# A shared expert with its weights held in the array and 512 tokens moving, and softmax sums collected in 128 columns

## The chip, the cores and the metric

The kernel runs on one core of one Trainium2 chip. The metric is the device time of one execution in microseconds (us), of which the median of several runs is given. All data are float32.

## What is computed

A transformer block for 2048 tokens of width 512. Its output is the input plus two branches, both of which read the layer-normalised input `xn`:

```
x  = query                                    # 2048 x 512
xn = layernorm(x)
# attention: 16 heads, two score matrices of depth 16 each, causal
a1, a2 = softmax(mask(q1 k1^T / 4)) v, softmax(mask(q2 k2^T / 4)) v      # v is 32 wide
f  = lowpass over tokens (a1 - lambda a2)     # filter in the frequency domain
attn = (rmsnorm per head(f) * const) @ Wout
# mixture of experts: 8 routed experts of width 352, the best 2 per token, and a shared one of width 704
routed = sum over the 2 chosen e:  w_e * ((silu(xn w1_e) * (xn w3_e)) @ w2_e)
shared = (silu(xn sw1) * (xn sw3)) @ sw2
out = x + attn + routed + shared
```

## The kernel before

Tokens lie in 16 tiles of 128. `xnT` holds the normalised input transposed (width on the partitions, in four chunks of 128, tokens along the free axis), `vd` the values. The work stands in three stages.

**First stage** (to about 259 us in the profile). Layer norm, transposes and the values; gating (which scatters a list `who` with 32 indirect DMAs, L400); the projections of queries and keys, which are written to memory as `parts_q` and `parts_k`; and last the shared expert for the first four token tiles (`EARLY = 4`), whose results go to memory as `ysh` (L199) on POOL's queue.

**Middle** (`middle`, 259 to 1313 us). Attention in 32 turns: 8 groups of two heads times 4 chunks of 512 queries. A turn is a list of units; a unit is one block of 128 keys for one head: two score matmuls (`ps_s`, L689), an exp on ACT over 128x1024 (`pt`, L702), and for both heads together four value matmuls into 32 columns each (`ps_o`, L733) and additions on DVE that collect the exps (`sum`, L743). When a turn has ended, `sums` adds `sum` over its partitions with matmuls against ones (`ps_sum`, L753), DVE copies the result (`s_sb`), and one step later `finish` transposes outputs and sums (`ps_ot`, `ps_st`, four transposes each) and DVE divides. Keys and queries come back from memory as `kS` (L597) and `qS` (L609) on SP's queue: four `kS` and eight `qS` transfers are needed for the first unit pair of the first turn.

Between the units, the generator `experts()` puts expert work into PE's queue: first the shared expert for token tiles 4 to 14, then 36 blocks of the routed experts. Each `yield` gives its cost by hand, and the loop takes as many steps as keep `worked / work_all` level with the share of attention units done. In this stage the order of PE, POOL and SP is the order in which the program is written; DVE and ACT are ordered by a scheduler.

**Ending** (1313 to 1432 us). The filter as matmuls on folded values (`ps_z`), the shared expert for the last token tile (`kept`), rms norm on DVE, the output projection (`po`), and sums of all parts by accumulating DMAs on POOL's queue.

**The shared expert before** is treated as two halves of width 352, each like a routed expert. For one token tile and one half, `up_first` does 4 matmuls (the tile's 128x128 chunks of `xnT` are the weights in the array, 352 columns of sw1 move; `xh`), a tanh on ACT and a DVE step that make silu; `up_third` does 4 more matmuls for sw3 (`xg`) and a product on DVE. The hidden values then lie with tokens on the partitions, so `turned_back` transposes them (three transposes, `ps_u`, L180, and two DVE copies, `uT`) before `down` multiplies with sw2 (`xy`, L190, 3 matmuls of 512 columns for each half). One float32 matmul is two PE instructions.

**Branches.** A branch on a flag `more` (L1140), whose body does up to three more routed blocks, stands in the text between the first stage and the middle; the scheduler places it into the streams. On the path where its body is not run, each engine only raises its counters by what the body would have raised. A second branch (L1157, `calm`) chooses between two forms of the middle; this input takes the first.

Matmul results go to `PSUM` banks of a pool `fps` with three buffers in the middle, which expert work, `ps_sum`, `ps_ot` and `ps_st` share in turn.

Of the kernel before, what the change touches and what calls it, by code (L numbers as in the profile page):

```python
# [8 lines left out]
F32 = mybir.dt.float32  # L9
# [10 lines left out]
P = 128  # L20
# [13 lines left out]
NF = len(FCH)  # L34
TOP = 2
# [24 lines left out]
def block_kernel(  # L60
# [41 lines left out]
    nc.vector.memset(ones, 1.0)  # L102
    calm = cpool.tile([1, 1], I32, name="calm")
# [34 lines left out]
    def expert(mp, fps, stores=2):  # L138


# [55 lines left out]
        def stored(y, dst, scale, eng=nc.sync):  # L196
            y_sb = mp.tile([P, E], F32, tag="y_sb", name="y_sb", bufs=stores)
            nc.vector.tensor_scalar(y_sb, y, scale, None, ALU.mult)  # L198
            eng.dma_start(dst, y_sb)  # L199
# [4 lines left out]
        return up_first, up_third, up, turned_back, (down, down_products, stored), transposed  # L204


    with ExitStack() as pools:
# [213 lines left out]
        _, _, up, turned_back, (down, _, _), _ = expert(ep, eps, EARLY)  # L421
# [49 lines left out]
        early = None  # L471
        for t in range(EARLY):
            xT = xnT[:, :, t * P : (t + 1) * P]
            u0 = up(w_sb[0][0], xT)
            if t == 0:
                pm = lps.tile([P, 2, P], F32, tag="x", name="ps_most")
                for i in range(2):
                    nc.tensor.transpose(pm[:1, i, :], most[:, i : i + 1], ident)
                line = l1.tile([1, 2], F32, name="line")
                nc.vector.tensor_reduce(line, pm[:1], AX.X, ALU.max)  # L480
                prod = l1.tile([1, 1], F32, name="prod")
                nc.vector.tensor_mul(prod, line[:, 0:1], line[:, 1:2])
                nc.vector.tensor_scalar(calm, prod, BOUND / (D * SCALE), None, ALU.is_le)
            else:
                early.append(turned_back(u1))
            u1 = up(w_sb[1][0], xT)
            if t > 0:
                down([(w[1], uT) for w, uT in zip(w_sb, early)], ysh[t - 1], 0.5, nc.gpsimd)
            early = [turned_back(u0)]
        early.append(turned_back(u1))  # L490
        down([(w[1], uT) for w, uT in zip(w_sb, early)], ysh[EARLY - 1], 0.5, nc.gpsimd)

    def middle(general):


        with ExitStack() as pools:
# [23 lines left out]
            up_first, up_third, _, turned_back, (down, _, _), transposed = expert(mp, fps)  # L520

            def experts():


                late = None
                for t in range(EARLY, NT - 1):
                    last = t == NT - 2
                    xT = xnT[:, :, t * P : (t + 1) * P]
                    half = up_first(w_sb[0][0], xT)
                    if t == NT - 3:  # L530
                        who_sb = mp.tile([NR, P, 2], F32, tag="who", name="who_sb", bufs=1)
                        nc.sync.dma_start(who_sb, who[: NR * P, :].rearrange("(n p) o -> n p o", p=P))
                    yield 2.4
                    u = up_third(w_sb[0][0], xT, half)
                    if last:


                        xr = [rows_of(0), rows_of(1)]
                        es = [routed(0)]
                        fetch_up(es[0], 0, nc.sync)  # L540
                    yield 2.4
                    uTs = [turned_back(u)]
                    half = up_first(w_sb[1][0], xT)
                    yield 2.9
                    u = up_third(w_sb[1][0], xT, half)
                    if last:
                        es.append(routed(1))
                        fetch_up(es[1], 1, nc.sync)
                    yield 2.4
                    if late is not None:  # L550
                        down(*late)
                    uTs.append(turned_back(u))
                    late = [(w[1], uT) for w, uT in zip(w_sb, uTs)], ysh[t], 0.5
                    if t == NT - 3:
                        ps = bank([P, 2, NR], "ps_w")
                        for i in range(2):
                            nc.tensor.transpose(ps[:, i, :], who_sb[:, :, i], ident[:NR, :NR])
                        nc.vector.tensor_copy(tok, ps[:, 0, :])
                        nc.vector.tensor_copy(wcol, ps[:, 1, :])
                    if last:  # L560
                        xT = transposed(xr.pop(0))
                    yield 5.7 if t > EARLY else 0.5
                for j in range(NR):
# [9 lines left out]
                    down(*late)  # L573
                    if j == 0:
                        fetch_down(es[0], 0, nc.sync)
                    fetch_down(es[j + 1], (j + 1) % 2, nc.sync)
# [82 lines left out]
            class Chunk:  # L659
# [88 lines left out]
                def sums(self):  # L748
                    ps = bank([P, QC], "ps_sum")
                    for h in range(2):  # L750
                        for s in range(2):
                            r = 64 * h + 32 * s
                            nc.tensor.matmul(  # L753
                                ps[r : r + 32, :], ones[:, :32], self.sum[h][:, s, :], start=True, stop=True,
                                skip_group_check=True,
                            )
                    self.s_sb = ap.tile([P, QC], F32, tag="s_sb", name="s_sb", bufs=1)
                    nc.vector.tensor_copy(self.s_sb, ps)

                def finish(self):  # L760
                    po = bank([P, TQ, 4, 32], "ps_ot")
                    psum = bank([P, TQ, 4, 32], "ps_st")
# [3 lines left out]
                    for i in range(TQ):  # L766
                        c = slice(i * P, (i + 1) * P)
                        nc.tensor.transpose(psum[:, i].rearrange("p a d -> p (a d)"), self.s_sb[:, c], ident)
                    r = ap.tile([P, TQ, 2, 2], F32, tag="rcp", name="rcp")
                    nc.vector.reciprocal(r.rearrange("p t h s -> p t (h s)"), psum[:, :, :, 0])  # L770
# [74 lines left out]
            work_all = (NT - 1 - EARLY) * 15.8 + NR * 8.5 - 7.0  # L845
# [78 lines left out]
    def ending():  # L924
# [3 lines left out]
        with tc.tile_pool(name="tail1", bufs=1) as t1, tc.tile_pool(name="tail", bufs=2) as tp, tc.tile_pool(  # L928
# [7 lines left out]
            up_first, up_third, _, turned_back, (_, down_products, stored), _ = expert(tp, fps)  # L936
# [67 lines left out]
            u = up_third(w_sb[0][0], kept, up_first(w_sb[0][0], kept))  # L1004
# [9 lines left out]
            uTs = [turned_back(u)]  # L1014
# [92 lines left out]
            half = up_first(w_sb[1][0], kept)  # L1107
# [3 lines left out]
            u = up_third(w_sb[1][0], kept, half)  # L1111
            pairs.append(prepared(1))
            uTs.append(turned_back(u))
            pairs[0].means()
            y = down_products([(w[1], uT) for w, uT in zip(w_sb, uTs)])
# [90 lines left out]
def _experts(w1, w3, w2, sw1, sw3, sw2):  # L1206
# [4 lines left out]
    halves = [slice(i * FI, (i + 1) * FI) for i in range(2)]  # L1211
    w1 = [*w1, *(sw1[:, h] for h in halves)]
    w3 = [*w3, *(sw3[:, h] for h in halves)]
    w2 = [*w2, *(sw2[h] for h in halves)]
    a = np.zeros((NX + 2, P, WCOL), np.float32)
    for e in range(NX + 2):
        up = a[e, :, : NE * 2 * FI].reshape(P, NE, 2, FI)
        for i, w in enumerate((w1[e], w3[e])):
            up[:, :, i] = w.reshape(NE, P, FI).transpose(1, 0, 2)
        for ic, (i0, m) in enumerate(FCH):  # L1220
            o = NE * 2 * FI + ic * E
            a[e, :m, o : o + E] = w2[e][i0 : i0 + m]
    return a
# [34 lines left out]
```

## Time and profile before

| | us |
|---|---|
| median of 3 runs (lowest to highest) | 1432.54 (1431.59 to 1432.81) |
| the profiled execution | 1433.46 |
| its span, from first to last instruction | 1431.7 |

| engine | busy us | share of the span |
|---|---|---|
| PE (matmul) | 1359.2 | 95% |
| DVE | 1073.6 | 75% |
| ACT | 660.7 | 46% |
| POOL | 568.7 | 40% |

The profile is of one execution. A group of instructions is given as line, engine, operation and tiles (output<-inputs), its shape and its count; a count of PE is of instructions, twice the matmuls for float32. "Idle before" is the time its engine waited, with what ended the wait. PEld is the loading of weights into the array, which overlaps matmuls; SPq and POOLq are the queues that issue DMAs.

### The profile page before, as it was taken

How to read it: one execution, taken by the hardware profiler on the slowest of the kernel's cores; microseconds unless marked ns; L12 is line 12 of the kernel's file. 1: busy time of each engine (PE TensorE's matmuls, PEld its weight loads, DVE VectorE, ACT ScalarE, POOL GpSimd, SP SyncE). 2: the span in 40 equal slices, each digit the busy share in tenths (PEclk: the TensorE clock that was granted, in tenths of full speed). 3: DMA queues.
4: the chain of work that ended last, by engine and by line, in shares of the span. 5: the costliest groups of instructions: out<-in, count | busy, mean ns of one | idle time of the engine just before them, and what ended most of it. 6: DMA issues, size and time to landing. Idle time of an engine off the chain costs nothing.

```text
span 1431.7 us, 19747 instructions
## 1 busy us (share of the span) xinstructions
PE 1359.2 (95%) x6968; PEld 637.4 (45%) x6968; DVE 1073.6 (75%) x1489; ACT 660.7 (46%) x780; POOL 568.7 (40%) x668
## 2 busy tenths in 40 slices
PE   7999999899999999999999999999989999999998
PEld 3444455344444443444444444444434444444443
DVE  7058872577777777777787889788879878887785
ACT  2211110455545545555565565556646546552221
POOL 0002222011301131136964754556548536623773
PEclk9999999999999999999999999999999999999999
DMA  9306661210101110236566656465566564546996
GB/s 378 145 15 206 185 197 33 74 56 33 61 28 37 38 62 14 60 126 177 181 190 180 218 179 185 143 208 180 157 177 198 185 179 157 174 153 234 194 223 147
DMA packets 74636, 206.51 MB, mean 144 GB/s; under 512 B 12012, under 2 KB 12176, under 8 KB 69152
## 3 DMA queue, kind: packets, MB, share of 16 engines
q1 hardware_dynamic: 61840, 177.62, 38.4%
q0 software_dynamic: 11168, 23.17, 8.0%
q10 hardware_dynamic: 1520, 4.36, 0.9%
q8 instruction: 58, 0.95, 0.3%
q14 instruction: 50, 0.41, 0.1%
HBM read 161.26 MB, written 43.85 MB: 143 GB/s over the span
## 4 chain that ended last, share of the span: by engine, by line
PE 58%; DVE 10%; POOL 5%; issue 5%; ACT 4%; DMA 3%; SPq 0%; ACTq 0%; DVEq 0%; POOLq 0%
PE ps_o L733 14%; PE ps_s L689 10%; PE xh L156 9%; PE xg L156 9%; PE xy L190 8%; DVE sum L743 4%; ACT pt L702 3%; PE ps_sum L753 2%; POOL pt L707 2%; DMA wd<-in_wex_dram 1%; PE po L1095 1%; DMA wu<-in_wex_dram 1%; PE ps_u L180 1%; DVE y_sb L198 1%; PE ps_ot L765 1%
## 5 line engine op out<-in xcount | busy, mean ns | idle before, releaser
L743 DVE TENSOR_TENSOR sum<-sum,pt 128x1024 f32<-128x1024 f32 (+3 forms) x576 | 627.4, 1123 | 111.9 <-ACT pt L702 61.7
L702 ACT ACTIVATE pt<-ps_s 128x1024 f32<-128x1024 f32 x544 | 533.6, 1026 | 256.8 <-PE ps_s L689 217.4
L707 POOL TENSOR_SCALAR_AFFINE_SELECT pt<-pt 128x256 f32<-128x256 f32 x256 | 160.3, 649 | 366.6 <-ACT pt L702 365.5
L733 PE MATMUL ps_o<-pt,vd 128*32 128x512 f32 (+3 forms) x2560 | 271.6, 542 | 1.9 <-POOL pt L707 1.9
L689 PE MATMUL ps_s<-qS,kS 64*128 64x512 f32 (+3 forms) x1280 | 214.5, 416 | 18.8 <-ACT pt L702 18.8
L190 PE MATMUL xy<-wd,uT 128*128 128x512 f32 (+1 forms) x408 | 186.8, 599 | 1.9 <-DMA wd<-in_wex_dram 1.5
L689 PEld LDWEIGHTS ps_s<-qS,kS 64*128 64x128 f32 x1280 | 100.3, 186 | 196.2 <-ACT pt L702 94.3
L733 PEld LDWEIGHTS ps_o<-pt,vd 128*32 128x32 f32 x2560 | 67.6, 110 | 133.8 <-issue 118.7
L782 POOL TENSOR_TENSOR vd<-o_n 128x128 f32<-128x128 f32 x62 | 34.9, 583 | 205.0 <-DVE o_n L773 144.7
L400 POOL DMA_INDIRECT who<-pairs,slot x32 | 36.2, 1132 | 196.5 <-DVE pairs L397 106.5
L190 PEld LDWEIGHTS xy<-wd,uT 128*128 128x128 f32 (+1 forms) x408 | 74.6, 190 | 86.5 <-issue 74.7
L446 PE MATMUL ps_x<-xnT,wqk_sb 128*128 128x512 f32 x256 | 110.5, 593 | 0.0
L163 ACT ACTIVATE xtanh<-xh 128x352 f32<-128x352 f32 x68 | 31.6, 464 | 146.1 <-PE xh L156 134.3
L156 PE MATMUL xh<-wu,xT 128*128 128x352 f32 x288 | 93.6, 468 | 1.3 <-DMA wu<-in_wex_dram 0.7
L156 PE MATMUL xg<-wu,xT 128*128 128x352 f32 x288 | 93.4, 467 | 0.0
L156 PE MATMUL xg<-wu,xnT 128*128 128x352 f32 x240 | 77.3, 464 | 0.8 <-DVE xtanh L164 0.6
L156 PE MATMUL xh<-wu,xnT 128*128 128x352 f32 x240 | 77.0, 464 | 1.0 <-DVE rcp L770 1.0
L149 ACT COPY xT<-ps_x 128x512 f32<-128x512 f32 x36 | 21.1, 586 | 118.6 <-PE ps_x L147 118.6
L446 PEld LDWEIGHTS ps_x<-xnT,wqk_sb 128*128 128x128 f32 x256 | 48.4, 190 | 60.6 <-issue 60.6
L156 PEld LDWEIGHTS xg<-wu,xT 128*128 128x128 f32 x288 | 52.7, 190 | 35.8 <-issue 9.6
L741 DVE COPY sum<-pt 128x1024 f32<-128x1024 f32 x64 | 49.7, 802 | 23.7 <-ACT pt L702 9.0
L156 PEld LDWEIGHTS xh<-wu,xT 128*128 128x128 f32 x288 | 51.8, 190 | 31.9 <-DVE sum L743 5.6
(230 smaller groups left out, 1437.5 us busy)
## 6 DMA issues: line engine op xcount, KB each, us to landing
wu<-in_wex_dram SPq DMA_DIRECT2D x40, 1408.0 KB
wd<-in_wex_dram SPq DMA_DIRECT2D x39, 768.0 KB
kS<-parts_k SPq DMA_DIRECT2D x128, 128.0 KB
qS<-parts_q SPq DMA_DIRECT2D x256, 64.0 KB
ys<-y_sb SPq DMA_DIRECT2D x36, 256.0 KB
parts_q<-hi SPq DMA_DIRECT2D x32, 256.0 KB
parts_k<-hi SPq DMA_DIRECT2D x16, 256.0 KB
parts_k<-turned SPq DMA_DIRECT2D x16, 256.0 KB
```

Source lines behind the costliest of these rows:

```text
L156: nc.tensor.matmul(dst, xT[:, c, :], w[:, o : o + FI], start=(c == 0), stop=(c == NE - 1))
L163: nc.scalar.activation(s, h, AF.Tanh, scale=0.5)
L190: nc.tensor.matmul(y, uT[:m, ic, :], w[:m, ic * E : (ic + 1) * E], start=(n == 0 and ic == 0), stop=(n == len(pairs) - 1 and ic == NF - 1),)
L400: nc.gpsimd.indirect_dma_start(out=who, out_offset=bass.IndirectOffsetOnAxis(ap=slot[:, k, t : t + 1], axis=0), in_=pairs[:, k, t, :], in_ ...
L446: nc.tensor.matmul(ps[:, i, :], wqk_sb[st, qk][:, i, c, :], xnT[:, c, cols], start=(c == 0), stop=(c == NE - 1),)
L689: nc.tensor.matmul(to, k, queries[2 * g + h, qc][r, off : off + w], start=True, stop=not general)
L702: nc.scalar.activation(pt[:, :, used], ps[:, :, used], AF.Exp, scale=SCALE)
L707: nc.gpsimd.affine_select(out=part, in_=part, pattern=[[0, 2], [1, P]], compare_op=ALU.is_ge, fill=0.0, base=0, channel_multiplier=-1,)
L733: nc.tensor.matmul(self.o[r : r + 32, off:], vd[:, kb, v0 : v0 + 32], pt[:, s, :], start=first, stop=self.ended, skip_group_check=True,)
L741: nc.vector.tensor_copy(to, pt)
L743: nc.vector.tensor_add(to, to, pt)
L782: eng.tensor_add(vd[:, self.qc * TQ : (self.qc + 1) * TQ, v0 : v0 + 32], self.o_n[:, :, h, 0, :], self.o_n[:, :, h, 1, :],)
```

## The change

The shared expert is no longer two halves of 352. Its width 704 is cut into eleven chunks of 128 columns: five of sw1 and five of sw3 in turn, and one that holds the last 64 of both. A chunk of the weights is held in the array and up to 512 tokens move past it, so the hidden values come out with width on the partitions, as the product with sw2 needs them, and are not transposed. The sixth slice of hidden values has 64 rows; it is kept in `u_last`, whose other half is zeroed once. For four token tiles there are 44 matmuls of 512 columns and then 24 of 512 (`result`). The groups of tiles are 0 to 3 (first stage), 4 to 7, 8 to 11, 12 to 14 (384 columns), and the last tile alone in the ending, with 44 matmuls of 128 columns. The weights are packed anew on the host to fit.

The sums of probabilities of a turn are collected in one 128x128 tile: 16 matmuls of 128 columns against `pick`, which has ones in one column of 32, take the place of 4 of 512; the copy takes 128 columns and one transpose takes the place of four.

In `experts()` the loads for the routed experts move: list and gathers into the last group of tiles, both `fetch_down` right after the shared expert; the costs in `yield` and `work_all` are new.

```diff
+    pick = cpool.tile([P, TQ, 32], F32, name="pick")
+    nc.gpsimd.memset(pick, 0.0)
+    for i in range(TQ):
+        nc.gpsimd.memset(pick[:, i, i : i + 1], 1.0)
+    u_last = [cpool.tile([P, QC], F32, name=f"u_last{i}") for i in range(2)]
+    for u in u_last:
+        nc.gpsimd.memset(u[P // 2 :, :], 0.0)
...
+    def shared_expert(mp, fps, places=SCH):
+        def hidden(k, x, dst=None):
+            if dst is None:
+                dst = fps.tile([P, x.shape[2]], F32, tag="f", name="wh")
+            for c in range(NE):
+                o = (NE * k + c) * P
+                nc.tensor.matmul(
+                    dst, w_sb[o // WUP][0][:, o % WUP : o % WUP + P], x[:, c, :], start=(c == 0), stop=(c == NE - 1)
+                )
+            return dst
+        def gated(h):
+            m = h.shape[0]
+            s = mp.tile([P, QC], F32, tag="ws", name="ws")
+            s = s[:m, : h.shape[1]]
+            nc.scalar.activation(s, h, AF.Tanh, scale=0.5)
+            nc.vector.scalar_tensor_tensor(s, s, 1.0, h, ALU.add, ALU.mult)
+            return s
+        def times(g, s, u=None):
+            if u is None:
+                u = mp.tile([P, QC], F32, tag="wu", name="wu_t", bufs=places)
+            nc.vector.tensor_mul(u[: g.shape[0], : g.shape[1]], g, s)
+            return u
+        def chunks(x, last):
+            us = []
+            for i in range(SCH - 1):
+                s = gated(hidden(2 * i, x))
+                yield us
+                us.append(times(hidden(2 * i + 1, x), s))
+                yield us
+            h = hidden(2 * SCH - 2, x)
+            us.append(times(h[P // 2 :, :], gated(h[: P // 2, :]), last))
+            yield us
+        def result(us, t, which=range(SCH), y=None):
+            if y is None:
+                y = fps.tile([P, E], F32, tag="f", name="wy")
+            for i in which:
+                nc.tensor.matmul(
+                    y, us[i][:, t * P : (t + 1) * P], w_sb[i // NF][1][:, i % NF * E : (i % NF + 1) * E],
+                    start=(i == 0), stop=(i == SCH - 1),
+                )
+            return y
...
-        early = None
-        for t in range(EARLY):
...
-            u0 = up(w_sb[0][0], xT)
...
-        early.append(turned_back(u1))
-        down([(w[1], uT) for w, uT in zip(w_sb, early)], ysh[EARLY - 1], 0.5, nc.gpsimd)
+        for n, us in enumerate(chunks(xnT[:, :, : EARLY * P], u_last[0])):
...
+        for t in range(EARLY):
+            stored(result(us, t), ysh[t], 0.5, nc.gpsimd)
...
-                for t in range(EARLY, NT - 1):
...
+                for t0 in range(EARLY, NT - 1, TQ):
+                    t1 = min(t0 + TQ, NT - 1)
+                    last = t1 == NT - 1
+                    for n, us in enumerate(chunks(xnT[:, :, t0 * P : t1 * P], u_last[t0 // TQ % 2])):
...
+                        yield 3.45 * (t1 - t0) / TQ
...
+                    for t in range(t0, t1):
+                        y = result(us, t - t0, range(NF))
+                        yield 2.6
+                        stored(result(us, t - t0, range(NF, SCH), y), ysh[t], 0.5)
+                        yield 2.6
...
+                for i in range(2):
+                    fetch_down(es[i], i, nc.sync)
...
-                    ps = bank([P, QC], "ps_sum")
...
-                                ps[r : r + 32, :], ones[:, :32], self.sum[h][:, s, :], start=True, stop=True,
+                    ps = bank([P, P], "ps_sum")
+                    for i in range(TQ):
+                        for h in range(2):
+                            for s in range(2):
+                                r = 64 * h + 32 * s
+                                nc.tensor.matmul(
+                                    ps[r : r + 32, :], pick[:, i, :], self.sum[h][:, s, i * P : (i + 1) * P],
+                                    start=(i == 0), stop=(i == TQ - 1), skip_group_check=True,
+                                )
...
-                    for i in range(TQ):
-                        c = slice(i * P, (i + 1) * P)
-                        nc.tensor.transpose(psum[:, i].rearrange("p a d -> p (a d)"), self.s_sb[:, c], ident)
+                    nc.tensor.transpose(psum, self.s_sb, ident)
...
-            work_all = (NT - 1 - EARLY) * 15.8 + NR * 8.5 - 7.0
+            work_all = (NT - 1 - EARLY) * ((2 * SCH - 1) * 3.45 / TQ + 5.2) + NR * 8.5 - 7.0
...
-            u = up_third(w_sb[0][0], kept, up_first(w_sb[0][0], kept))
+            us = times(several((1, 3)), gated(several((0, 2))))
...
+            h = several((4, 6, 8, 10))
+            s = gated(h)
...
+            u = times(several((5, 7, 9)), s[:, : 3 * P])
...
-            y = down_products([(w[1], uT) for w, uT in zip(w_sb, uTs)])
+            y = result(us, 0)
```

`several(ks)` runs `hidden` for the chunks `ks` on `kept` into one bank, 128 columns each.

## The prediction

> **What bounds the kernel now.** I read the page's first line, then busy time by stage, then PE's waits, then the two seams between stages.
>
> ```profile
> PE 1359.2 (95%) x6968; PEld 637.4 (45%) x6968; DVE 1073.6 (75%) x1489; ACT 660.7 (46%) x780; POOL 568.7 (40%) x668
> ```
>
> PE is the bound, so PE work taken away counts unless a wait takes its place. The table by window (PE, PEld, DVE, ACT, POOL busy; clock; DMA share; GB/s) shows where:
>
> ```profile
> 196.00:259.00 63.00, 61.78 (x202) 35.28 (x200) 22.37 (x46) 4.75 (x9) 15.42 (x17) 1.00 0.29 90
> 259.00:625.00 366.00, 346.55 (x1973) 159.78 (x1976) 275.37 (x355) 198.22 (x221) 64.92 (x101) 1.00 0.15 50
> 625.00:1313.00 688.00, 660.28 (x3977) 308.22 (x3970) 562.87 (x692) 392.30 (x450) 394.89 (x478) 0.99 0.57 178
> ```
>
> The early shared expert (196 to 259) is PE from end to end. From 259 to 625, where the rest of the shared expert runs, PE idles 19.5 of 366; from 625 on DVE is busy 82% and PE 96%. The waits of PE between 266 and 625 say what those idles are:
>
> ```profile
> PE ps_s L689 <- ACT pt L702: 9.5, 18, 0.9
> PE ps_u L180 <- DVE xu L171: 7.3, 5, 2.7
> ```
>
> The second is the transposes of the shared expert waiting for its DVE product. Now the seam between first stage and middle. First PE's timeline, then SP's queue, then SP's wait, then PE and POOL at the `more` branch:
>
> ```profile
> 252.60 0.82 PE L180 MATMUL ps_u<-cst,xu 128*128 128x128 f32 x6
> 253.87 5.42 PE L190 MATMUL xy<-wd,uT 128*128 128x512 f32 x12 [0.46 <-DVE uT L182]
> 259.23 0.73 PE L689 MATMUL ps_s<-qS,kS 64*128 64x512 f32 x4
> ```
> ```profile
> 238.50 3.28 SPq L597 DMA_DIRECT2D kS<-parts_k  x4
> 241.83 13.84 SPq L609 DMA_DIRECT2D qS<-parts_q  x8
> ```
> ```profile
> SPq L597 <- DMA who<-pairs,slot: 26.0, 1, 26.0
> ```
> ```profile
> L1140 PEldq EVENT_SEMAPHORE  x1: 51/51/51, 210.4 to 210.4; - x1
> L1140 POOLq INC_SWDGE_SEM  x1: 857/857/857, 237.4 to 237.4; - x1
> ```
>
> SP stands 26 us at its first `kS` load, whose wait includes counters that each engine raises at the `more` branch. PE passes the branch at 210.4, POOL, behind its `who` scatters, at 237.4; one us later the load goes out. The four `kS` land at 245.4, 249.8, 252.6 and 255.4, the last of the first `qS` at 257.2. So the load chain takes 18.7 us from its first issue, and ends 2 us before PE's last early matmul. It is just hidden.
>
> **The change part by part.**
>
> *Price of PE work.* One instruction of 512 columns takes 430 ns in a full stream (860 a float32 matmul), one of 352 takes 296, one of 128 takes 107 to 109: 0.84 ns a column, almost nothing fixed.
>
> *Shared expert, products.* Before, one token tile needed 16 matmuls of 352 columns, 16×0.592 = 9.47; now 44 of 512 serve four tiles, 44×0.86/4 = 9.46. Down is 6×0.86 = 5.16 in both. Equal.
>
> *Shared expert, transposes.* Two triples of `ps_u` a tile go. A triple takes 0.32 where PE streams (237.31 to 237.64) and 0.43 in the middle, where weights change (1302.53 to 1302.95 around one). Early: 44×0.86+24×0.86 = 58.5 from 195.8, plus the 1.2 of idle in that window, is 255.4 for the end of the last `wy`, against 259.0: −3.6. Middle: 11 tiles, 22×0.43 = −9.5. With them goes the wait for `xu`, 7.3: some returns as `wy` waiting for the last product, and I take −5.5 (bounds −7.3 and 0).
>
> *Sums.* 16 matmuls in four column groups instead of 4: 32 instructions, eight steps of four groups side by side. At 0.109 a step that is 0.87, against two steps of 430 = 0.86 before. The nearest row is `ps_o`, which has the same 32-column groups: 32 instructions from 1306.62 to 1308.91 take 2.29 where pure streaming would take 2.15. The Trainium skill, "TensorEngine Tiling (Array Packing)", section Instruction Overhead, speaks against it: each matmul costs some 60 cycles and one should not cut a dimension that is small already. If a fixed cost came on top of each, at the 25 ns that 60 cycles are at 2.4 GHz, 24 more instructions in 32 turns would be +19 us (an estimate from that page). The row has 107 to 109 ns for 128 columns, all of it streaming, so I take zero, and leave +19 as the far bound; with it the sum would be +12, a case I give no more than 1 in 50 (inside D's chance). Three of four `ps_st` transposes go: 3×0.108×32 = −10.4. DVE saves about 0.4 on each of 32 copies of `s_sb` (689 ns each) and some 15 us on `uT`; it is not the bound, so this is nothing in itself.
>
> *Middle in sum.* 9.5+5.5+10.4 = 25.4. PE is 95 to 96% busy there, so some of what is saved turns into waits for `pt` or `sum`. Also, a bank of three is now held across a `yield` by the half-finished `wy`, which can make `ps_sum` wait. Times 0.92: −23.3 (from −17 to −26).
>
> *Ending.* `kept` has 88 instructions of 128 columns, 88×0.109 = 9.6 against 9.47; four chunks gated at once let DVE finish about 1 later: +1. Leftover expert work at the end of the middle fills an idle of 1.4 there: −1. Together zero. If the weight load (190 ns for 128×128) did not hide behind 107 ns of streaming, 88×0.08 = +7; the same on `ps_sum` (weights 32 wide, 110 ns) is nearly nothing.
>
> *What is moved and costs nothing.* The memsets of `pick` and `u_last` stand at POOL's head, before a load needed 60 us later. `who_sb`, `rows_of` and `fetch_up` come earlier on SP and POOL, many units ahead of use. Both `fetch_down` stand on SP waiting for the last shared matmul, with later `kS`/`qS` loads queued behind; these are wanted about 19 us later. If that slack is gone, it costs as much as the longest wait for `wd` now, 1.5.
>
> *The new wait.* The scheduler places the branch. In the order of the changed program PE's part of `more` stands after all 24 `wy` matmuls; the old program has the early expert's last 50 us behind it. SP's first `kS` load waits for PE's counter at that branch. So it is issued not at 238.5 but when PE has ended, about 255.6, and the loads that were hidden are now bare. They take 18.7 as seen; the first two used 11.3 of it beside other traffic, and were they as quick as the third and fourth (2.8 each, plus 2 to start, an estimate), 15.0. I take 17.0, so the first scores come at 272.6 instead of 259.2: **+13.4** (from +11.4 to +15.1), the saved 3.6 already in it. That nothing else can fill PE follows from the program order: the shared expert's next step stands behind the first scores.
>
> *A cold PE.* After 7.9 us of idle at the start, the profile shows this:
>
> ```profile
> 9.70 6.76 PE L291 MATMUL ps_tv<-wv_sb,xnT 128*128 128x512 f32 x8 [0.68 <-ACT xnT L288]
> 17.63 7.13 PE L291 MATMUL ps_tv<-wv_sb,xnT 128*128 128x512 f32 x16
> ```
>
> Eight instructions in 6.76 against sixteen in 7.13: half speed for some 6 to 7 us, a loss of 3.2. The skill's "TensorE: Matmul & The Clock Gate", Part 1, gives half clock after an idle window of about 3.4 us, until about 3.4 us of activity: a loss of 1.7. An idle of 17 is long enough for either. By the row the sum gains 3.2, by the rule 1.7; the first units also wait for ACT (1.5 us in before), which hides part. I take +2.5 (0 to 3.6).
>
> *Sum.* −23.3 + 13.4 + 2.5 + 0 = −7.4. The profiled execution took 1433.46, so 1426.1; the median of the runs is 0.9 lower: about **1425**.
>
> **The rivals.**
>
> *A, the forecast, 0.67*: transposes gone, half given back at the seam. Own range 1417 to 1430.
>
> *B, the seam is free, 0.09*: the counter is raised by PE's sequencer ahead of its matmuls, or the waits resolve otherwise, so the loads go out near 238. For: the trace shows PE's branch read at 207 while PE streams. Against: the load waits for a count that includes the matmuls before the branch. Then −3.6−23.3: 1432.5−26.9 = 1405.6.
>
> *C, no difference, 0.13*: the loads take 18.7, the clock 3.6, the middle yields only 17, since DVE is busy 82% from 625 on: −17+15.1+3.6 = +1.7, some 1434 down to 1430.
>
> *D, slower, 0.11*: the same load chain, bare. After the first four `kS` seven more are issued at once (in the profile from 255.72, 10.5 us of issuing) and every later unit of the first turns needs them; before, they ran behind PE. If they come late too, PE stops again after each block, and the start loses not 16 but more than the 23.3 that the middle gains; it decides from there, and beyond what a measurement tells from 26 on. A late block of `kS` is 2.8 by the landings above: with three, −23.3+16+8.4 = +1; with four +4, about 1436; with four and the middle at −20, +7, about 1440. Against: eight matmuls, an exp and four products a unit give the loads about as long as they need.
>
> That the change does not do what it says would be the transposes staying; the program's order has none, so no chance is given to it.
>
> **How the numbers follow.** The range holds A, most of C and part of D and reaches toward B: 1411 to 1435. About 0.2% (2.9 us) is what a measurement of this kernel can tell from no change. Faster than 1429.6: nearly all of A (0.64), B (0.09), 0.02 of C: 0.75. Within: 0.03 of A, 0.09 of C, 0.02 of D: 0.14. Slower than 1435.4: the rest of C and D, 0.11.
>
> **What would show it.** Right: the first `kS` issue within a us after the last `wy` near 255; PE idle about 17 us there with the wait put down to `qS` or `kS`; some 6 us of doubled durations after it; `ps_u` down from 204 transposes (three for each of 68 half tiles or routed blocks) to 108, `ps_st` from 128 to 32; `ps_sum` no dearer than 35 us busy in all; the rest of the middle shorter by 20 to 25. Wrong: a `kS` issue before 245 (then B); PE idle again between 275 and 300 (then D); `ps_sum` steps well over 0.11 (then the rule about small dimensions was right); PE's total busy time down, yet idle up by as much after 625 (then DVE had become the bound).

## The result, and the profile after

The changed kernel takes 1413.93 us (median of 4 runs, 1413.75 to 1418.09), against 1432.67 for the kernel before in the same comparison: a ratio of 0.9875 (95% interval 0.9855 to 0.9896). A second comparison, made with the last experiments, gave 0.9857 (0.9837 to 0.9878). The prediction had the sign, with 1425 and a range of 1411 to 1435; the gain is 18.7 where it said 7.4.

The first line of the page and the head of its group of costs, of the kernel after:

```profile
span 1411.9 us, 20669 instructions
...
PE 1340.1 (95%) x7472; PEld 619.3 (44%) x7472; DVE 1055.9 (75%) x1414; ACT 660.5 (47%) x774; POOL 583.1 (41%) x675
```

PE is 19.1 less busy, and that looks like the whole gain of 19.8 in the span. It is not, as the seam shows. PE's timeline of the kernel after:

```profile
252.24 1.02 PE L266 MATMUL wy<-wd,u_last 128*128 128x512 f32 x2
270.03 1.62 PE L748 MATMUL ps_s<-qS,kS 64*128 64x512 f32 x4 [16.77 <-DMA qS<-parts_q]
272.24 1.71 PE L748 MATMUL ps_s<-qS,kS 64*128 64x512 f32 x4 [0.58 <-ACT pt L761]
273.88 5.06 PE L229 MATMUL wh<-xnT,wu 128*128 128x512 f32 x8
```

and SP's timeline, then the instructions of the `more` branch (now L1210) on PE:

```profile
253.43 2.33 SPq L656 DMA_DIRECT2D kS<-parts_k  x4
```
```profile
L1210 PEldq TENSOR_LOAD <-more x1: 489/489/489, 245.4 to 245.4; - x1
...
L1210 PEldq EVENT_SEMAPHORE  x1: 51/51/51, 253.3 to 253.3; - x1
```

The new wait of 16.8 is there. PE's queue reads the flag 8 us before its matmuls end, but it raises the counter only behind the last `wy`, at 253.3; the first `kS` load leaves at 253.4. So PE lost 17 us and still gained 20: some other idle time must have gone. The table by window (as in the prediction: PE, PEld, DVE, ACT, POOL busy, clock, DMA share, GB/s) of the kernel after shows where:

```profile
194.51:253.26 58.75, 58.75 (x139) 25.74 (x137) 18.10 (x26) 4.62 (x7) 13.99 (x15) 1.00 0.24 77
...
270.03:625.00 354.97, 350.02 (x2115) 145.40 (x2115) 270.28 (x311) 204.22 (x224) 63.83 (x100) 0.99 0.18 60
625.00:1296.09 671.09, 643.31 (x4388) 313.75 (x4385) 559.75 (x701) 386.08 (x442) 409.38 (x478) 0.99 0.57 179
1296.09:1411.90 115.81, 104.32 (x322) 51.18 (x320) 82.20 (x145) 26.64 (x42) 69.43 (x48) 0.96 0.92 200
```

From the first score to 625, PE idles 355.0 − 350.0 = 5 us. The kernel before idled 19.5 in that stretch. PE's waits from 271 to 640 in the kernel after are two lines:

```profile
PE ps_s L748 <- ACT pt L761: 4.5, 11, 0.6
PE xh L168 <- ACT xT L161: 0.7, 1, 0.7
```

The wait of `ps_u` for `xu` has gone with its transposes. That was foreseen. The wait of the scores for `pt`, in an engine and on a line that the change does not touch, fell from 11.0 (between 260 and 625 before) to 4.5, or 4.2 in that same window. That was not.

Taking the first `ps_s` and `ps_r` as the limits of the middle, the profiled executions compare so:

| | before | after | difference | prediction |
|---|---|---|---|---|
| first score of the middle | 259.23 | 270.03 | +10.8 | +13.4 |
| middle, to `ps_r` | 1060.1 | 1026.1 | −34.1 | −23.3 + 2.5 |
| of it PE busy | 1011.5 | 993.3 | −18.2 | −19.9 + 2.5 |
| of it PE idle | 48.6 | 32.7 | −15.9 | −5.5 + 2.0 |
| ending | 112.3 | 115.8 | +3.5 | 0 |
| span | 1431.7 | 1411.9 | −19.8 | −7.4 |

In the last column the prediction's factor of 0.92, which takes 2.0 off the gain, is put to the idle time.

### The profile page after: what moved, and what is told of

Same layout as the page of the kernel before. It is cut to its first block, busy times and chain, and to the rows that moved or that the text cites. A ratio compares the mean times of both kernels' runs of the same rounds, so it can differ in the third digit from the quotient of the medians.

```text
span 1411.9 us, 20669 instructions
## 1 busy us (share of the span) xinstructions
PE 1340.1 (95%) x7472; PEld 619.3 (44%) x7472; DVE 1055.9 (75%) x1414; ACT 660.5 (47%) x774; POOL 583.1 (41%) x675
## 4 chain that ended last, share of the span: by engine, by line
PE 59%; DVE 6%; POOL 5%; DMA 5%; issue 3%; ACT 3%; SPq 0%; ACTq 0%; DVEq 0%; POOLq 0%
PE ps_o L792 16%; PE ps_s L748 11%; PE wh L229 8%; PE xg L168 5%; PE xh L168 5%; PE xy L202 5%; PE wy L266 4%; POOL pt L766 3%; ACT pt L761 2%; DVE sum L802 2%; PE ps_sum L814 2%; DMA kS<-parts_k 2%; DMA wd<-in_wex_dram 1%; POOL res L1019 1%; PE po L1163 1%
## 5 line engine op out<-in xcount | busy, mean ns | idle before, releaser
L802 DVE TENSOR_TENSOR sum<-sum,pt 128x1024 f32<-128x1024 f32 (+3 forms) x576 | 638.1, 1141 | 117.5 <-ACT pt L761 62.1
L766 POOL TENSOR_SCALAR_AFFINE_SELECT pt<-pt 128x256 f32<-128x256 f32 x256 | 163.2, 661 | 341.0 <-ACT pt L761 339.9
L748 PE MATMUL ps_s<-qS,kS 64*128 64x512 f32 (+3 forms) x1280 | 214.9, 417 | 30.6 <-DMA qS<-parts_q 16.8
L229 PE MATMUL wh<-xnT,wu 128*128 128x512 f32 (+1 forms) x352 | 151.0, 577 | 0.0
L843 POOL TENSOR_TENSOR vd<-o_n 128x128 f32<-128x128 f32 x62 | 41.4, 688 | 189.5 <-DVE o_n L834 121.1
L202 PE MATMUL xy<-wd,uT 128*128 128x512 f32 (+1 forms) x216 | 100.9, 603 | 0.6 <-DVE rcp L829 0.6
L229 PEld LDWEIGHTS wh<-xnT,wu 128*128 128x128 f32 x352 | 64.8, 191 | 71.9 <-issue 54.2
L266 PE MATMUL wy<-wd,wu_t 128*128 128x512 f32 x160 | 73.6, 601 | 0.0
L1019 POOL DMA_INDIRECT res<-ys,slot x32 | 54.7, 1711 | 22.3 <-DMA res<-ysh 11.5
```

The costliest lines, as they stand in the source:

```text
L202: nc.tensor.matmul(y, uT[:m, ic, :], w[:m, ic * E : (ic + 1) * E], start=(n == 0 and ic == 0), stop=(n == len(pairs) - 1 and ic == NF - 1),)
L229: nc.tensor.matmul(dst, w_sb[o // WUP][0][:, o % WUP : o % WUP + P], x[:, c, :], start=(c == 0), stop=(c == NE - 1))
L266: nc.tensor.matmul(y, us[i][:, t * P : (t + 1) * P], w_sb[i // NF][1][:, i % NF * E : (i % NF + 1) * E], start=(i == 0), stop=(i == SCH - 1),)
L748: nc.tensor.matmul(to, k, queries[2 * g + h, qc][r, off : off + w], start=True, stop=not general)
L766: nc.gpsimd.affine_select(out=part, in_=part, pattern=[[0, 2], [1, P]], compare_op=ALU.is_ge, fill=0.0, base=0, channel_multiplier=-1,)
L802: nc.vector.tensor_add(to, to, pt)
```

## The experiments

Ratios are to the kernel before on the same chip, each with its 95% interval. Spans, waits and stages are of the one profiled execution of each kernel. "Middle" is always from the first `ps_s` to `ps_r`.

### The two parts alone

`e1_sums` is the kernel before with this, and `pick`, as its only change:

```diff
-                    ps = bank([P, QC], "ps_sum")
...
+                    ps = bank([P, P], "ps_sum")
+                    for i in range(TQ):
...
+                                    ps[r : r + 32, :], pick[:, i, :], self.sum[h][:, s, i * P : (i + 1) * P],
...
+                    nc.tensor.transpose(psum, self.s_sb, ident)
```

> The kernel before with the new sums alone (16 matmuls of 128 columns, a copy of 128 columns, one transpose of sums a turn). Theory B (the PE time of the prediction, 1:1, nothing besides): three transposes of 32 turns, -10.4, so 1422. The prediction's own factor gives -9.6. Theory W (waits shrink as well, because DVE carries some 13 us less and its bank comes free earlier): -13 to -17, so 1416 to 1420, with PE's idle between 625 and 1313 smaller by 3 or more.

Measured: 1428.61, ratio 0.9967 (0.9958 to 0.9975), so −4.7: less than either theory. The middle is 2.9 shorter. PE is 7.7 less busy in it (1011.5 to 1003.8), but its idle time grew from 48.6 to 53.4. The waits of PE that grew are for transfers and for a bank (total, times, longest):

```profile
PE xh L161 <- DMA wu<-in_wex_dram: 3.0, 1, 3.0
PE ps_x L152 <- DVE y_sb L203: 3.0, 6, 0.6
PE xy L195 <- DMA wd<-in_wex_dram: 2.6, 1, 2.6
```

In the kernel before these three are 0.7, 1.1 and 1.5. Theory W, that DVE's relief would shrink other waits, fell: DVE is 11 less busy in the middle, and PE waits more.

`e2_shared` is the kernel after with the old sums (the ones are taken from the tile of constants, to make room):

```diff
+    ones = cst[:, C_TRI + P : C_TRI + 2 * P]
...
-                    ps = bank([P, P], "ps_sum")
+                    ps = bank([P, QC], "ps_sum")
...
+                    for i in range(TQ):
+                        c = slice(i * P, (i + 1) * P)
+                        nc.tensor.transpose(psum[:, i].rearrange("p a d -> p (a d)"), self.s_sb[:, c], ident)
```

> The kernel after with the old sums (4 matmuls of 512, copy of 512, four transposes); only the shared expert and its moved loads are new. If the two parts add, it lies at about -18.7 less what e1 shows. Theory B: +13.4+2.5-3.6... that is the seam as measured (+10.8), middle -9.5-5.5, ending +3.5: about 1432. Theory W: the shared expert frees PE from all of its waits between 260 and 625, 19.5 us of idle down to about 5, so that the middle yields some 24 and the run lies at about 1423.

Measured: 1422.78, ratio 0.9932 (0.9912 to 0.9953), on the value of theory W. PE's idle time in the middle is 32.8, the same as in the kernel after (32.7). So all of the −15.9 comes with the shared expert and none with the sums. The sums, put on top of it, take 9.2 off the middle (1035.3 to 1026.1), all of it busy time; alone they took 2.9.

### Is it DVE's load?

`e4_dve_load` is the kernel after with additions that nothing reads:

```diff
             nc.vector.tensor_mul(u[: g.shape[0], : g.shape[1]], g, s)
+            if mp.name == "shared" and g.shape[0] == P:
+                for _ in range(4):
+                    w = s.shape[1] // 2
+                    nc.vector.tensor_add(junk[:, :w], s[:, :w], s[:, w:])
...
                     nc.vector.tensor_copy(self.s_sb, ps)
+                    idle_dve(2, self.sum[0][:, 0, :])
```

> The kernel after with DVE work added that nobody uses: in each product of the shared expert in the middle four additions of 256 columns (15 times about 1.2 us), after each turn's sums two (32 times about 0.6 us): some 35 us on DVE, about what the change took off it in the middle. Theory R (relief of DVE made PE's other waits shrink): the time rises by 6 to 12. Theory S (the handshakes of the transposes went, and the load of DVE does not matter): it rises by less than 3.

Measured: 1421.21, ratio 0.9924 (0.9901 to 0.9947), +7.3 against 1413.93. The windows of this run, with the same columns, say where. (Its profiled execution is the fastest of six, 1418.15, and shows 4.5 of the 7.3.)

```profile
269.43:625.00 355.57, 350.67 (x2119) 145.79 (x2120) 295.91 (x391) 204.76 (x225) 64.70 (x100) 0.99 0.18 60
625.00:1303.13 678.13, 644.00 (x4383) 314.98 (x4381) 573.69 (x744) 385.58 (x442) 405.76 (x478) 0.99 0.56 176
```

To 625 DVE carries 25.6 more than in the kernel after, and PE idles 4.9, as there: in the stage whose idle time the prediction got wrong, DVE's load does nothing. From 625 on DVE carries 13.9 more, and PE's idle rises from 27.8 to 34.1. Theory R fits the routed stage and is wrong for the shared one. Of the −15.9, −14.9 lies in the shared stage (before the first matmul of a routed block, idle falls from 19.8 to 4.9); so DVE's load does not explain it.

### Is it the order and the size of the steps?

`e6_swap`, on the kernel before:

```diff
-                    uTs = [turned_back(u)]
                     half = up_first(w_sb[1][0], xT)
+                    uTs = [turned_back(u)]
                     yield 2.9
```

> The kernel before, with only the order of two things in a step of the shared expert changed in the middle: the next half's four matmuls first, then the three transposes that wait for DVE's product. Theory S1 (the wait ps_u for xu is worth its 7.3): -6 to -7.5, the wait of ps_s for pt stays at 11. Theory S2 (that wait covered another, and PE meets it next): -0 to -3. The prediction took 5.5.

Measured: 1427.44, ratio 0.9961 (0.9948 to 0.9974), or −5.6 by the ratio, between the two theories and close to S1. In its trace the wait of `ps_u` for `xu` falls from 7.3 to 2.8 and that of `ps_s` for `pt` stays at 11.4:

```profile
PE ps_s L689 <- ACT pt L702: 11.4, 21, 1.1
PE ps_u L180 <- DVE xu L171: 2.8, 2, 2.5
```

So 4.5 of the wait went, PE's idle time in the middle fell by 5.1, and no other wait took its place: the mechanism is that of S1. The profiled execution hides this in its span, which is only 0.8 shorter. It is the slowest of the nine (1432.65), at a mean granted clock of 0.988 against 0.993, and PE is 4.9 longer busy in its middle.

`e7_swap_split` adds to it the division of sw2's 12 matmuls:

```diff
                     if late is not None:
-                        down(*late)
+                        pairs, *to = late
+                        y = down_products(pairs, (0,))
+                        yield 2.6
+                        stored(down_products(pairs, (1,), y), *to)
...
-                    yield 5.7 if t > EARLY else 0.5
+                    yield 3.1 if t > EARLY else 0.5
```

> e6 with the 12 matmuls of sw2 in two steps of 6 with units between, as the kernel after does. Theory L (the wait of ps_s for pt, 11.0 before and 4.5 after between 260 and 625, comes from uneven steps: units that get a long step and units that get none): a further -4 to -6, idle of PE between 260 and 625 down to about 7. Rival (it comes from the load of ACT or DVE): no change against e6.

Measured: 1421.51, ratio 0.9915 (0.9898 to 0.9932), some 6 more. The wait for `pt` is now close to that of the kernel after, with the shared expert in its old form and all its transposes:

```profile
PE ps_s L694 <- ACT pt L707: 5.1, 11, 1.1
PE ps_u L180 <- DVE xu L171: 2.8, 2, 2.4
```

The sum of both is −12.2 by the ratio, without one instruction less on PE. The rival fell too: in the shared stage DVE and ACT are as busy in e7 (282.5 and 206.1) as before (282.9 and 205.2). One place shows how it comes about, here in the kernel before:

```profile
302.14 5.32 PE L190 MATMUL xy<-wd,uT 128*128 128x512 f32 x12
...
310.24 0.79 PE L689 MATMUL ps_s<-qS,kS 64*128 64x384 f32 x8
311.86 0.50 PE L689 MATMUL ps_s<-qS,kS 64*128 64x256 f32 x4 [0.83 <-ACT pt L702]
312.78 0.57 PE L689 MATMUL ps_s<-qS,kS 64*128 64x512 f32 x2 [0.41 <-ACT pt L702]
```

and here in e7, where the second half of the 12 stands between the same scores:

```profile
301.17 2.74 PE L192 MATMUL xy<-wd,uT 128*128 128x512 f32 x6
...
306.35 0.79 PE L694 MATMUL ps_s<-qS,kS 64*128 64x384 f32 x8
307.07 2.84 PE L192 MATMUL xy<-wd,uT 128*128 128x512 f32 x6
...
310.17 0.73 PE L694 MATMUL ps_s<-qS,kS 64*128 64x256 f32 x6
```

The cause of the unforeseen part is so shown: with a step of 5.7 in one gap between units, other gaps have none, and there PE comes back to the scores before ACT has made room. ACT's exp takes 1.03 for a full unit and PE's scores 0.73, so PE runs ahead where the scores of several units follow each other with no expert work between; even steps of 2.6 to 3.4 cover most of it.

`e8_lump` is the reverse, on the kernel after:

```diff
-                        y = result(us, t - t0, range(NF))
-                        yield 2.6
-                        stored(result(us, t - t0, range(NF, SCH), y), ysh[t], 0.5)
-                        yield 2.6
+                        stored(result(us, t - t0), ysh[t], 0.5)
+                        yield 5.2
```

> The kernel after with the 6 matmuls of sw2 for a tile in one step of 5.2 instead of two of 2.6. Theory L: PE's wait of ps_s for pt in the shared stage rises from 4.5 to 7 to 9 and the time by 2 to 5. Rival: within 1.5 of the kernel after.

Measured: 1416.35, ratio 0.9878 (0.986 to 0.9897), which the kernel after's own 0.9875 does not separate from it. The trace does: the wait for `pt` in the shared stage is back at 7.8 from 4.5, as theory L said, and the span is 2.8 longer. The effect is shown in the trace and is too small to be shown in the times.

### Is PE's work paid one to one, and what are the sums worth?

`e11_pe_load`, the kernel after with transposes that wait for nothing new:

```diff
+                if mp.name == "shared":
+                    for i in range(2):
+                        nc.tensor.transpose(dst[:, i * P : (i + 1) * P], ident, ident)
...
-                    nc.tensor.transpose(psum, self.s_sb, ident)
+                    for i in range(TQ):
+                        nc.tensor.transpose(psum[:, i, :], self.s_sb, ident)
```

> The kernel after with transposes of 128 columns added that nothing reads: two ahead of each chunk of the shared expert in the middle (66), and three more of the sums in each turn (96). They wait for nothing new. Theory (what PE does is paid 1:1, at 0.108 to 0.144 each): +17 to +22. Rival (part of it disappears in waits that PE has anyway): +8 to +14.

`e12_after_again` is the kernel after once more, beside e9, e10 and e11:

> The kernel after itself on the same chip, as the measure for e9 and e11: 0.985 to 0.990 of the kernel before, by every theory.

Measured: e11 takes 1428.3 (0.9957, 0.994 to 0.9973) against 1412.89 for the kernel after in the same comparison: +15.4 for 162 transposes, 0.095 each. That lies between the two theories' ranges, and the times alone do not tell them apart. The traces do. In the middle PE is 14.9 longer busy than in the kernel after, 0.092 for each transpose where the theory took at least 0.108, the middle is 14.0 longer, and PE's idle time is 0.9 less. So the work was cheaper than expected, and it is paid nearly one to one.

`e10_split_sums` puts the new sums of e1 on e7:

> e7 (the kernel before with transposes one step later and sw2 in two steps) with the new sums. The sums were worth 4.7 on the kernel before and about 8 on top of the new shared expert. Theory M (alone they lose some to the loads of the routed weights, which the kernel before issues later, and this wait grows as the middle shortens): -2 to -5 against e7, waits for wu and wd 4 to 6 together. Rival (they lose it to the waits of the shared expert): -8 to -10 against e7.

Measured: 1418.07, ratio 0.9888 (0.9868 to 0.9907), −3.9 against e7 by the ratios, whose intervals just overlap. The size is that of theory M, its mechanism is not: the waits for `wu` and `wd` are 3.7 together, and 4.0 in e7. Of PE's waits, what grew from 1.1 and 0.4 is

```profile
PE ps_x L152 <- DVE y_sb L205: 3.3, 6, 0.6
PE ps_o L743 <- POOL pt L717: 2.5, 3, 1.6
```

So on the kernel before, and on e7, the new sums are worth 4 to 5, and with the new shared expert and its moved loads about 9. The times at which a bank comes free and a mask is done have shifted against PE; which of the moved steps prevents that was not tried, and stays open.

### The seam

`e3_seam` writes the early shared expert behind the branch, in a pool of its own above 40 kB of the memory that the middle takes first:

```diff
+    early(10000)
+
     flag = nc.values_load(calm[0:1, 0:1], min_val=0, max_val=1)
```

> The kernel after with the early shared expert written behind the branch `more`, in memory of its own, so that PE passes the branch before it and the first kS load need not wait for the last wy. Theory (the stall is the load chain made bare): first kS issue at about 238 as in before, chain of 18.7 ends at 257, PE idle of 16.8 falls to about 4, the cold clock goes too: -13 to -15 against the kernel after, about 1400. Rival (some other counter or memory holds the loads): issue stays at 253, no gain. Rival (PE stands at the branch): the gain is less by what it waits there, 2 to 4.

Measured: 1436.82, ratio 1.0027 (1.0014 to 1.0039), a loss of 23 against the kernel after. PE did pass the branch early, but met two waits (its timeline), the first of them foreseen with a smaller size:

```profile
203.40 5.19 PE L230 MATMUL wh<-xnT,wu 128*128 128x512 f32 x8 [7.75 <-DVEq L1218]
...
234.53 34.17 PE L230 MATMUL wh<-xnT,wu 128*128 128x512 f32 x72 [22.28 <-DVE ws L241]
```

The wait at the seam itself went as the theory said: the first `kS` load leaves at 236.7, and the first scores wait 1.0. But the two waits cost more than that. The second is a chain. DVE waits for ACT's `ws`, and ACT, by its waits, for the `who` scatters:

```profile
ACT ws L240 <- DMA who<-pairs,slot: 31.3, 1, 31.3
```

The early pool had come to lie where the scatters' lists or the branch's own tiles lie. That only the place in memory, and nothing in the data, joins them was read from the program, and was not tried by itself.

`e5_first_loads` moves the loads instead of the work:

```diff
-            kp, qp, pp = pool("k", 2), pool("q", 2), pool("prob", 5 if general else 6)
+            kp, qp = pool("k", 2), pool("q", 2)
...
+            load_keys(0, 0)
+            load_queries(0, NQC - 1)
+            rest()
+            pp = pool("prob", 5 if general else 6)
```

`rest()` is the `more` branch, moved into the middle.

> The kernel after with the first kS and qS loads of the middle ahead of the branch `more`, which now stands inside the middle behind them, before the other memory of the middle is taken. The first load then waits only for the last ps_x (PE, near 195) and the stores of parts_k. Theory (the 16.8 of PE's wait at the seam is the load chain made bare by the branch): issue near 209, all loads landed by 230, PE goes on within 2 us of the last wy, the cold clock goes: -16 to -18.5 against the kernel after, 1395 to 1398. Rival (the seam has another wait close behind, of the branch itself, of POOL or of later keys, as in e3): less than half of it.

Measured: 1402.68, ratio 0.9784 (0.9771 to 0.9798): 10 to 13 us below the kernel after by its two ratios, and so below both kernels. The first load leaves at 209.15, and PE goes on at 256 (SP's timeline, then PE's):

```profile
209.15 3.03 SPq L589 DMA_DIRECT2D kS<-parts_k  x4
```
```profile
253.02 1.02 PE L266 MATMUL wy<-wd,u_last 128*128 128x512 f32 x2
256.00 0.84 PE L771 MATMUL ps_s<-qS,kS 64*128 64x512 f32 x4 [1.96 <-DMA kS<-parts_k]
259.06 1.71 PE L771 MATMUL ps_s<-qS,kS 64*128 64x512 f32 x4 [2.22 <-ACT pt L784]
```

So the seam was the load chain made bare. Of the 16 to 18.5 expected, some 3 to 8 are missing. Two waits of some 2 us are left, and the half clock with them (0.50 between 258 and 264). Also the ending is 119.0 long, 3.2 longer than in the kernel after.

`e9_pace` is e5 with one more change, aimed at that ending:

```diff
-            work_all = (NT - 1 - EARLY) * ((2 * SCH - 1) * 3.45 / TQ + 5.2) + NR * 8.5 - 7.0
+            work_all = (NT - 1 - EARLY) * ((2 * SCH - 1) * 3.45 / TQ + 5.2) + NR * 8.5 - 1.0
```

> e5 with work_all 6 larger, so that the expert steps run ahead and fewer are left over at the end of the middle (the hand-given costs add up to 10.3 more than work_all in after and e5, 4.6 more in before). Theory (the ending of after is 3.5 longer and that of e5 6.7 because the last routed block ends late: its y_sb is still being stored when ACT needs the memory for the first gate of the last tile, and DVE and PE stand behind that): the wait of ps_z for vd falls from 3.5 to below 1, and the time by 2 to 4 against e5. Rival (the steps are missed elsewhere, or the memory was not it): within 1 of e5, or slower by the 1.4 of idle before ps_r.

Measured: 1402.38, ratio 0.9769 (0.975 to 0.9789), not to be told from e5. In the trace the theory holds for the ending, which falls from 119.0 to 112.3; PE's wait of `ps_z` for `vd` falls from 3.5 to 0.4. But this execution lost nearly as much at the start: in the shared stage PE idles 12.3, in e5 6.6. Its timelines of PE and of POOL, and POOL at the branch:

```profile
264.60 1.71 PE L771 MATMUL ps_s<-qS,kS 64*128 64x512 f32 x4 [7.92 <-ACT pt L784]
```
```profile
252.90 0.96 POOL L468 DMA_INDIRECT who<-pairs,slot  x1 [4.32 <-DMA who<-pairs,slot]
258.52 0.96 POOL L468 DMA_INDIRECT who<-pairs,slot  x1 [4.66 <-DMA who<-pairs,slot]
```
```profile
L554 POOLq INC_SWDGE_SEM  x1: 936/936/936, 262.2 to 262.2; - x1
```

The scatters of `who`, one after another on POOL, took 2.4 us apiece in the kernel after between 215 and 228. Beside the key loads that now run from 226 on they take 5.3. In e5 that is so too, from 229 on, but at 212 seven scatters were still to come there, and here nine; the last one was at 245.7, here at 258.5. POOL raises its counter at the branch only behind them, at 262.2 for 0.9 (256.6 in e5). ACT's first `pt` begins 0.4 to 0.5 after that in both, at 263.5 and 258.0. That it waits for memory which this counter sets free is inferred; the traces put ACT's wait down to a load of keys or queries. That e9's starts are all like this one is not shown; its runs spread from 1398.55 to 1403.86. A version that holds the later keys back until the scatters are through was not tried.

## Why the prediction was wrong

- **The step that failed** is in "Middle in sum", in PE's idle time. The prediction counted one wait, that of `ps_u` for `xu`, at −5.5; it put the wait of the scores for `pt` at nothing gained, and then multiplied everything by 0.92, because "some of what is saved turns into waits for `pt` or `sum`". That made −3.5 of idle; −15.9 is measured. The wait for `pt`, far from growing, shrank.
- The term is 12.4 off, and the whole span is 12.4 off too, which is partly chance: against the prediction, the seam came 2.6 and PE's busy time 0.8 cheaper, and the ending 3.5 dearer.
- Of the 15.9, e6 shows 5.1 (idle in the middle 48.6 to 43.5) for the wait of `ps_u`, so that the 5.5 was about right, and e7 shows 6.4 more (to 37.1) for even steps. Of the remaining 4.4, about 4 lie in the shared stage (9.0 in e7, 4.9 after), where e7 still waits 2.8 for `xu`; the rest of it was not traced to a cause. The routed stage has nearly the same idle time in all three: 28.8 before, 28.1 in e7, 27.8 after. There the 4.0 that e7 waits for `wu` and `wd` is gone after, but other waits have come (`ps_st` for `s_sb`, 5.1); what the moved `fetch_down` is worth alone was not tried.
- The list of PE's waits had `ps_s` for `pt` on its first line, with 9.5, and the text passed over it to the second. The costs in the `yield`s, 2.4, 2.4, 2.9, 2.4 and 5.7 before, 3.45 and 2.6 after, stood in the programs: the change evens out the steps, and the prediction read them as bookkeeping.
- **PE's busy time** was right: −9.5 and −10.4, with 1.3 less of `kept` done before `ps_r` and 3.2 for the half clock, make −18.0; −18.2 is measured. `ps_sum` is 35.4 busy after and 35.3 before, with four times as many instructions. The prediction's far bound, a fixed cost of 60 cycles on top of each (its estimate from "TensorEngine Tiling (Array Packing)", Instruction Overhead, in the Trainium skill), would have made +19; with 128 columns and four column groups side by side none shows. But the value on the end, one to one, held only with the new shared expert (e2 to after, 9.2 in the middle), not alone (e1, 2.9).
- **The early stage**: 58.75 for 58.5, without the 1.2 of idle. PE also reached it 1.3 earlier, which no step of the change explains.
- **The new wait**: 16.8 for 17.0. Rival B fell: PE's queue does read the flag early, but the counter waits for the matmuls.
- **The cold PE**: the first instructions after the stall (1.62 and 1.71 for 0.73, 5.06 for 3.70) lose 3.2, the row's value; the prediction's estimate from the Trainium skill, "TensorE: Matmul & The Clock Gate", Part 1, half clock for some 3.4, would have made it 1.7. The clock was 0.50 from 262 to 274 and full by 278.
- **The ending**: 0 was said, +3.5 came. PE's idle time there is the same (11.4 before, 11.5 after); its busy time is 3.4 more, and two stretches of half clock account for that. Behind a wait of 1.99 for `vd`, 32 `ps_z` instructions take 15.67 (13.97 in e12, behind 1.17); behind one of 2.03 for `a`, 8 of `po` take 5.36 for 3.70. The prediction reckoned with a cold PE at the seam alone. In e12 only the second came, and the ending is 113.0, 0.7 longer than before. The step "leftover expert work fills an idle" was right on the idle, and silent on the last `y_sb`: ACT's first gate waits for its store (17.1), and the `vd` behind it comes late. With fewer steps left over (e9) the wait for `vd` is 0.4. That it is the store is not certain: in e5 the trace puts the same wait down to the load of `wo_sb`.
- **Rival D** did not come: after the stall PE idles 0.58 once before 279, and the later keys were in time.

## What to carry to other kernels

Where one engine's queue weaves two kinds of work, size is not all: an uneven filling leaves gaps in which the engine waits for another one, and that wait stands in the list under a line that no edit touches. So read every wait of the stage, not only the one that an edit names, and ask of each how the step lengths would change it. And before work is reordered near a branch, look for who waits for the counters raised at it: a load issued ahead of the branch was worth 10 to 13 us here, while the work moved behind it cost 23.

## What the runs showed of the hardware that was not expected

- A short wait of PE was followed by half clock in some places and not in others. In the ending of the kernel after it was, twice:

```profile
1303.39 15.67 PE L1035 MATMUL ps_z<-xnT,conv 128*128 128x512 f32 x32 [1.99 <-DVE vd L1081]
...
1340.30 1.09 PE L1155 MATMUL ps_tr<-cst,a 128*128 128x128 f32 x8 [2.03 <-DVE a L1128]
1341.63 5.36 PE L1163 MATMUL po<-wo_sb,aT 128*128 128x512 f32 x8 [0.24 <-ACT aT L1157]
```

  The granted clock is 0.63 from 1303.4 to 1306 and 0.60 from 1341 to 1344. A wait of 2.04 in e4 was not followed by it (3.70 for the eight `po`), nor was one of 2.08 in e9. In the kernel before it came behind two shorter waits, of the kind that even steps remove:

```profile
420.44 0.50 PE L689 MATMUL ps_s<-qS,kS 64*128 64x512 f32 x2 [0.88 <-ACT pt L702]
421.36 0.50 PE L689 MATMUL ps_s<-qS,kS 64*128 64x512 f32 x2 [0.41 <-ACT pt L702]
421.79 3.41 PE L733 MATMUL ps_o<-pt,vd 128*32 128x512 f32 x16
```

  The 16 `ps_o` take 1.92 elsewhere; the clock is 0.68 from 421 to 424. In these three places the half clock cost 1.5 to 1.7, about as much as the wait before it, and it stands in the table as busy time.
- Scatters that follow each other on POOL's queue went from 2.4 us apiece in the kernel after to 5.3 in e9, where key loads run beside them.
